# Talking-heads attention with a soft mixture of experts: another order of the mixing, the row transfers, the copies and the projection

## The chip, the cores and the metric

The kernel runs on one core of a Trainium2 chip. The metric is the device time of one execution in microseconds (us); lower is better. The engines are PE (TensorE: matmuls, with PEld for its weight loads), DVE (VectorE), ACT (ScalarE), POOL (GpSimd) and SP (SyncE, which here only issues transfers).

## The reference

There are 4 sequences of 2048 tokens with 256 features. The attention has 16 heads of 16 features and mixes the heads twice, once before the softmax and once after it. A soft mixture of experts follows; both have a residual and a norm behind them. The change touches the attention alone:

```python
qkv = x @ Wqkv.T + bqkv
q, k, v = jnp.split(qkv, 3, axis=-1)
...
q = apply_rope(q)
k = apply_rope(k)
logits = jnp.einsum('bhid,bhjd->bhij', q, k) * SCALE
logits = jnp.einsum('bhij,gh->bgij', logits, Wpre)
attn = jax.nn.softmax(logits, axis=-1)
attn = jnp.einsum('bhij,gh->bgij', attn, Wpost)
out = jnp.einsum('bhij,bhjd->bhid', attn, v)
out = out.transpose(0, 2, 1, 3).reshape(b, n, DIM)
return out @ Wout.T + bout
```

## The kernel before

For each sequence the kernel computes q, k and v (`qkv`), then the attention, then the experts (`moe`). All data is float32.

**The attention** takes the queries by pairs of blocks. A block has 8 queries (`IB`), so with 16 heads it fills 128 partitions; a pair `n` has two blocks, `x` = 0 and 1, and there are 128 pairs a sequence. The keys are split into two halves, `j` = 0 and 1, of 1024 (`HALF`), and into four quarters of 512 (`QN`).

A pair passes through four stages, spread over several steps of the loop in line 562:

1. `raw_banks(n, c, engs)`, lines 359 to 382: the products of q and k, before any mixing. It runs twice for a pair, for `c` = 0 and 1 (8 heads each). PE writes four PSUM tiles `s` (line 374). Each is copied into the SBUF tile `raw` by one of the functions that it returns: `fs[0]` to `fs[3]`. `V` copies on DVE (line 550), `S_` on ACT (line 553). `pair_q` (line 351) prepares the q side on POOL.
2. `raw_rows(n)`, lines 384 to 396: eight transfers on SP's queue of 256 KB each. They bring `raw` into four row tiles `raws[n][j][x]`, in which the heads lie on partitions. Row tiles have 10 buffers (`ROWS`), `raw` has two.
3. `logits(n, j)`, line 414: PE mixes the heads into two PSUM tiles `l`, one for each `x`. `top(n, j, x)`, line 429, takes the negative maximum of a row on DVE, and `expo(n, j, x)`, line 438, the exponential on ACT, back into the row tile, with the sum beside it. A maximum belongs to one half of the keys alone, so `shares(n)`, lines 444 to 457, works out the factors that join the halves: `m` on DVE (line 449), a subtraction on POOL (451), an exponential on ACT (452), a product and a sum on POOL (454, 456). `weights(n)`, lines 459 to 472, takes the reciprocal on DVE (463) and makes the mixing weights `w` from it on POOL (464, 466).
4. `mix(n, x, j, engs)`, line 495: PE mixes the heads again and turns the result at once, into two PSUM tiles `t` for one `x` and one `j`. `V` and `S_` copy them into `aT`. When 32 queries (four blocks, `GI`) are there, `values(grp, hf)`, line 519, multiplies with v in two parts, `hf` = 0 and 1, each in a step of its own, into a PSUM tile `o`. Two DVE instructions copy it (530, 531). After every fourth group, so in every eighth step, `finish(it)`, lines 537 to 547, projects 128 queries: it loads x (line 259, on SP's queue), adds the bias on POOL (540), multiplies on PE into `pz` (543), and adds and takes the statistics of the norm on DVE (546, 237).

**One step `n`** holds, for each half `j`: `logits(n, j)`, `raw_banks(n + 2, j, ...)`, the maxima and exponentials of pair `n`, and the mixing of pair `n - 1`. At its end it starts the row transfers of pair `n + 2` and multiplies with v for an earlier group.

[...]the tiles `l` have two buffers of two banks, and all the others (`s`, `t`, `o`, `pz`) share four buffers of one bank.

**The order of the work.** A scheduler places each instruction on its engine's queue by its own estimate of when the inputs are ready, so an instruction can stand elsewhere than the program has it. `keep(...)` stops that for one instruction: it stays behind everything that the program has before it on that engine. Before the change the copies `V` and `S_`, `top`, `expo` and the row transfers are kept; `shares`, `weights`, the copies of `o` and `finish` are not. PE's and POOL's instructions are placed freely in both kernels.

Of the kernel before, what the change touches and what calls it, by code (L numbers as in the profile page):

```python
# [16 lines left out]
P = 128  # L17
# [8 lines left out]
def kernel(  # L26
# [301 lines left out]
    def attention(b, y, qT, kT, v):  # L328
# [30 lines left out]
        def raw_banks(n, c, engs):  # L359
# [3 lines left out]

            if c == 0:
                raws[n] = {
                    "qb": pair_q(n),
                    "from": work.tile([P, HP, QN], F32, tag="raw", name=f"raw_{b}_{n}"),
                }
            qb = raws[n]["qb"]
            prs = [ps_t.tile([P, QN], F32, tag="t", name=f"s_{b}_{n}_{c}_{r}") for r in range(4)]  # L370
            for r in range(4):
                rows = slice(32 * r, 32 * (r + 1))
                for q in range(4):
                    nc.tensor.matmul(  # L374
                        prs[r][32 * q : 32 * (q + 1), :],
                        qb[rows, c, q % 2].rearrange("p s i h x -> p (s i h x)"),
                        kT[rows, c, ts(q, QN)],
                        start=True,
                        stop=True,
                    )  # L380
# [3 lines left out]
        def raw_rows(n):  # L384
# [7 lines left out]
            for x in range(2):  # L392
                for q in range(2):
                    for j in range(2):
                        p0 = 32 * (2 * j + q)
                        keep(nc.sync.dma_start(raws[n][j][x][:, ts(q, QN)], raw[p0 + x : p0 + 32 : 2]))  # L396
# [47 lines left out]
        def shares(n):  # L444
# [4 lines left out]
            nc.vector.tensor_tensor(m, m2[:, :, 0:1], m2[:, :, 1:2], ALU.min)  # L449
            f = small.tile([P, 2, 2], F32, tag="f", name=f"f_{b}_{n}")  # L450
            nc.gpsimd.tensor_tensor(f, m.to_broadcast([P, 2, 2]), m2, ALU.subtract)  # L451
            nc.scalar.activation(f, f, AF.Exp)  # L452
# [6 lines left out]
        def weights(n):  # L459
# [3 lines left out]
            nc.vector.reciprocal(z, z)  # L463
# [45 lines left out]
        outT = {}  # L509

        def values(grp, hf):
# [18 lines left out]
            nc.vector.tensor_copy(dst, po[:, 0, :])  # L530
            nc.vector.copy_predicated(dst, odd, po[:, 1, :])
            if hf == 1:
                aT.pop(grp)
                if part == P // GI - 1:
                    finish(it)

        def finish(it):
            oT = outT.pop(it)
            xt = load_x(b, it, "xr")
            nc.gpsimd.tensor_add(xt, xt, bout_sb)  # L540
# [5 lines left out]
            nc.vector.tensor_add(y[:, it, :], pz[:, :D], xt)  # L546
            norm_stats(y[:, it, :], it, st)
# [14 lines left out]
        for n in range(n_pairs + 3):  # L562
# [4 lines left out]
            for j in range(2):  # L567
# [7 lines left out]
                fs[0]()  # L575
                fs[1]()
# [3 lines left out]
                fs[2]()  # L580
                fs[3]()
                if cur:
                    expo(n, j, 1)
                if prv:
                    mix(n - 1, j, 0, (V, S_))
                    mix(n - 1, j, 1, (V, S_))
                    if j == 1:
                        state.pop(n - 1)
                if j == 1:
# [4 lines left out]
            if cur:  # L594
                shares(n)
        mv, rstd = norm_finish(st, f"a{b}")
# [190 lines left out]
```

## Time and profile before

| | us |
|---|---|
| median of 3 runs | 10179.63 |
| lowest, highest | 10157.14, 10192.11 |
| the profiled execution | 10203.34 |
| its span, first to last instruction | 10201.3 |

The granted clock of TensorE is 0.937 on average.

| engine | busy us | share of the span | instructions |
|---|---|---|---|
| PE | 7866.9 | 77% | 264788 |
| PEld | 5049.5 | 49% | 264788 |
| DVE | 5577.1 | 55% | 9074 |
| ACT | 4927.5 | 48% | 9758 |
| POOL | 1617.7 | 16% | 6478 |

The transfers of SP's queue take 44.6% of the time of the 16 DMA engines, and the queues that bring instructions 1.4% and 0.1%.

The profile names instructions by line, engine, output and inputs. A line of the timeline has the start, the duration, what ran and how often; in brackets behind it stand the idle time of that engine just before and what ended it. "issue" there means that the engine waited for nothing that the profile shows. A line of the list of waits has the engine with the work that waited, what it waited for, the sum in us, how often, and the longest. Each float32 matmul is recorded as two matmuls and two weight loads.

### The profile page before, as it was taken

How to read it: one execution, taken by the hardware profiler on the slowest of the kernel's cores; microseconds unless marked ns; L12 is line 12 of the kernel's file. 1: busy time of each engine (PE TensorE's matmuls, PEld its weight loads, DVE VectorE, ACT ScalarE, POOL GpSimd, SP SyncE). 2: the span in 40 equal slices, each digit the busy share in tenths (PEclk: the TensorE clock that was granted, in tenths of full speed). 3: DMA queues.
4: the chain of work that ended last, by engine and by line, in shares of the span. 5: the costliest groups of instructions: out<-in, count | busy, mean ns of one | idle time of the engine just before them, and what ended most of it. 6: DMA issues, size and time to landing. Idle time of an engine off the chain costs nothing. (4 is left out here: it accounts for less than half of the span.)

```text
span 10201.3 us, 569636 instructions
## 1 busy us (share of the span) xinstructions
PE 7866.9 (77%) x264788; PEld 5049.5 (49%) x264788; DVE 5577.1 (55%) x9074; ACT 4927.5 (48%) x9758; POOL 1617.7 (16%) x6478
## 2 busy tenths in 40 slices
PE   7887778776778787777677877787767787777776
PEld 4554555454455454545444545555544554545554
DVE  5555555554555555555455555555545555555554
ACT  3544555453455455545345545554534554555453
POOL 2111111111211111111121111111112111111111
PEclk9989999998999999999899999999989998999898
DMA  4444554452455454545244545554514554555441
GB/s 108 120 120 111 129 128 121 113 124 57 105 122 124 115 127 121 124 116 120 54 105 120 124 115 124 124 126 117 123 48 113 120 124 115 125 124 124 116 120 47
DMA packets 653638, 1150.99 MB, mean 113 GB/s; under 512 B 95616, under 2 KB 125440, under 8 KB 651264
## 3 DMA queue, kind: packets, MB, share of 16 engines
q1 hardware_dynamic: 616704, 1099.18, 44.6%
q8 instruction: 2076, 34.01, 1.4%
q10 hardware_dynamic: 34560, 15.36, 0.6%
q14 instruction: 298, 2.44, 0.1%
HBM read 32.13 MB, written 8.39 MB: 4 GB/s over the span
## 5 line engine op out<-in xcount | busy, mean ns | idle before, releaser
L495 PE MATMUL t<-w,rows 64*64 64x64 f32 x131072 | 3029.9, 233 | 877.9 <-ACT raw L553 566.4
L495 PEld LDWEIGHTS t<-w,rows 64*64 64x64 f32 x131072 | 2600.5, 144 | 2156.1 <-ACT raw L553 1067.5
L553 ACT COPY raw<-s 128x512 f32<-128x512 f32 x2552 | 1443.0, 589 | 3977.5 <-PE s L374 3460.3
L429 DVE TENSOR_REDUCE m<-l 128x1 f32<-128x1024 f32 x2048 | 2496.9, 1220 | 869.4 <-PE l L414 869.2
L438 ACT ACTIVATE rows<-l,m 128x1024 f32<-128x1024 f32 x2048 | 2311.7, 1129 | 111.9 <-DVE m L429 110.6
L374 PE MATMUL s<-kT,qb 32*32 32x512 f32 x32768 | 2029.2, 639 | 177.7 <-issue 162.1
L414 PE MATMUL l<-rows,wmix_sb 32*32 32x512 f32 x32768 | 1630.0, 636 | 307.3 <-issue 275.1
L550 DVE COPY aT<-t 128x512 f32<-128x512 f32 x2048 | 1359.0, 683 | 508.3 <-PE t L495 506.2
L519 PE MATMUL o<-aT,v 128*32 128x64 f32 x65536 | 1155.5, 223 | 619.4 <-issue 439.7
L519 PEld LDWEIGHTS o<-aT,v 128*32 128x32 f32 x65536 | 1006.4, 111 | 740.6 <-issue 500.6
L553 ACT COPY aT<-t 128x512 f32<-128x512 f32 x2048 | 1179.5, 601 | 395.2 <-PE t L495 381.0
L550 DVE COPY raw<-s 128x512 f32<-128x512 f32 x1544 | 1056.9, 685 | 524.9 <-PE s L374 512.8
L374 PEld LDWEIGHTS s<-kT,qb 32*32 32x32 f32 x32768 | 715.0, 106 | 979.1 <-issue 707.4
L351 POOL TENSOR_TENSOR qb<-qT,hmask 128x16 f32<-128x16 f32 (+3 forms) x3584 | 647.3, 220 | 1899.9 <-PE s L374 1899.9
L451 POOL TENSOR_TENSOR f<-m,m 128x4 f32<-128x4 f32 x512 | 101.7, 199 | 4532.3 <-DVE m L449 4531.5
L463 DVE RECIPROCAL z<-z 128x2 f32<-128x2 f32 x512 | 85.0, 166 | 1149.6 <-POOL z L456 1149.6
L414 PEld LDWEIGHTS l<-rows,wmix_sb 32*32 32x32 f32 x32768 | 328.9, 106 | 672.3 <-issue 513.4
L530 DVE COPY aoT<-o 128x32 f32<-128x32 f32 x512 | 98.3, 192 | 957.6 <-PE o L519 957.6
L438 ACT ACTIVATION_READ_ACCUMULATOR rows<-l,m 128x1 f32 x2048 | 433.5, 212 | 0.0
L466 POOL TENSOR_TENSOR w<-wblk_sb,f 128x256 f32<-128x256 f32 x512 | 313.7, 613 | 40.6 <-POOL f L464 1.0
L454 POOL TENSOR_TENSOR zf<-f,z 128x4 f32<-128x4 f32 x512 | 102.4, 200 | 751.9 <-ACT f L452 751.9
L309 POOL TENSOR_TENSOR s<-qk,wq 128x256 f32<-128x256 f32 x128 | 116.3, 928 | 494.1 <-DVE qk L293 481.4
(122 smaller groups left out, 2620.9 us busy)
## 6 DMA issues: line engine op xcount, KB each, us to landing
rows<-raw SPq DMA_DIRECT2D x4096, 256.0 KB
x<-in_x_dram SPq DMA_DIRECT2D x64, 128.0 KB
xr<-in_x_dram SPq DMA_DIRECT2D x64, 128.0 KB
out_dram<-qT SPq DMA_DIRECT2D x16, 512.0 KB
wm<-in_w_dram ACTq DMA_DIRECT2D x8, 512.0 KB
wm<-in_w_dram ACTq DMA_DIRECT2D x4, 1024.0 KB
wq<-in_wqkvT_dram ACTq DMA_DIRECT2D x4, 768.0 KB
wq<-in_bqkv_dram ACTq DMA_DIRECT2D x4, 384.0 KB
```

The source lines that it names most:

```text
L309: nc.gpsimd.tensor_mul(s[:, :, a, :], qk[:, :, 1 - a, :], ss[a])
L351: nc.gpsimd.tensor_tensor(qb[:, :, g, s0:s1, :, :, x].rearrange("p c s i h -> p c (s i) h"), qT[:, t, :, i0:i1].unsqueeze(3).to_broadcast( ...
L374: nc.tensor.matmul(prs[r][32 * q : 32 * (q + 1), :], qb[rows, c, q % 2].rearrange("p s i h x -> p (s i h x)"), kT[rows, c, ts(q, QN)], sta ...
L414: nc.tensor.matmul(pls[x][32 * c : 32 * (c + 1), ts(h, 512)], wmix_sb[32 * q : 32 * (q + 1), :], raws[n][j][x][32 * q : 32 * (q + 1), ts(h ...
L429: nc.vector.tensor_reduce(s["m2"][:, x, j : j + 1], s["l", j][x], AX.X, ALU.max, negate=True)
L438: nc.scalar.activation(s["e", j][x], s["l", j][x], AF.Exp, bias=s["m2"][:, x, j : j + 1], accum_out=s["z2"][:, x, j : j + 1],)
L454: nc.gpsimd.tensor_tensor(zf, f, z2, ALU.mult)
L466: nc.gpsimd.tensor_tensor(w, wblk_sb.rearrange("p g i -> p (g i)").unsqueeze(1).to_broadcast([P, 4, HEADS * IQ]), f.rearrange("p x j -> p ...
L495: nc.tensor.matmul(pts[r][64 * c : 64 * (c + 1), a, :], e[rows, k0 : k0 + 64], s["w"][rows, 2 * x + j, :], start=True, stop=True,)
L519: nc.tensor.matmul(po[32 * c : 32 * (c + 1)].rearrange("p a i -> p (a i)"), v[:, t, g0 * HD : (g0 + 2) * HD], at[:, t, g0 : g0 + 2, :].rea ...
L550: keep(nc.vector.tensor_copy(dst, src))
L553: keep(nc.scalar.copy(dst, src))
```

## The change

It has five parts.

- The q k products of `raw_banks` lie on other partition groups: the key quarters 0, 2, 1, 3 instead of 0, 1, 2, 3. `raw_rows` fits that and sends all of `j` = 0 first, then `j` = 1; before, all of `x` = 0 went first.
- The mixing of a half step takes both blocks `x` for one half `j`; before, it took one block for both halves.
- All four copies `fs` stand ahead of the first exponential and the second maximum. The first `mix` of a half step now stands between the two exponentials.
- More of the attention is kept in program order: `m` and the exponential of `shares`, the reciprocal of `weights`, the copies of `o`, and the addition and statistics of `finish`.
- `finish` runs in the middle of the step after the one whose `values` complete its 128 queries. Its load of x and the addition of the bias move into `values`, two steps ahead of it.

```diff
             for r in range(4):
                 rows = slice(32 * r, 32 * (r + 1))
                 for q in range(4):
                     nc.tensor.matmul(
                         prs[r][32 * q : 32 * (q + 1), :],
-                        qb[rows, c, q % 2].rearrange("p s i h x -> p (s i h x)"),
-                        kT[rows, c, ts(q, QN)],
+                        qb[rows, c, q // 2].rearrange("p s i h x -> p (s i h x)"),
+                        kT[rows, c, ts(2 * (q % 2) + q // 2, QN)],
...
-            for x in range(2):
-                for q in range(2):
-                    for j in range(2):
-                        p0 = 32 * (2 * j + q)
-                        keep(nc.sync.dma_start(raws[n][j][x][:, ts(q, QN)], raw[p0 + x : p0 + 32 : 2]))
+            for j in range(2):
+                for x in range(2):
+                    for h in range(2):
+                        p0 = 32 * (2 * h + j) + x
+                        keep(
+                            nc.sync.dma_start(
+                                raws[n][j][x][:, ts(h, QN)], raw[p0 : p0 + 31 : 2]
+                            )
+                        )
...
-            nc.vector.tensor_tensor(m, m2[:, :, 0:1], m2[:, :, 1:2], ALU.min)
+            keep(nc.vector.tensor_tensor(m, m2[:, :, 0:1], m2[:, :, 1:2], ALU.min))
...
-            nc.scalar.activation(f, f, AF.Exp)
+            keep(nc.scalar.activation(f, f, AF.Exp))
...
-            nc.vector.reciprocal(z, z)
+            keep(nc.vector.reciprocal(z, z))
...
-            nc.vector.tensor_copy(dst, po[:, 0, :])
-            nc.vector.copy_predicated(dst, odd, po[:, 1, :])
+            keep(nc.vector.tensor_copy(dst, po[:, 0, :]))
+            keep(nc.vector.copy_predicated(dst, odd, po[:, 1, :]))
+            if part == P // GI - 1 and hf == 0:
+                xs[it] = load_x(b, it, "xr")
+                nc.gpsimd.tensor_add(xs[it], xs[it], bout_sb)
             if hf == 1:
                 aT.pop(grp)
                 if part == P // GI - 1:
-                    finish(it)
+                    todo.append(it)
 
         def finish(it):
             oT = outT.pop(it)
-            xt = load_x(b, it, "xr")
-            nc.gpsimd.tensor_add(xt, xt, bout_sb)
...
-            nc.vector.tensor_add(y[:, it, :], pz[:, :D], xt)
-            norm_stats(y[:, it, :], it, st)
+            keep(nc.vector.tensor_add(y[:, it, :], pz[:, :D], xs.pop(it)))
+            keep(nc.vector.bn_stats(st[:, it, :], y[:, it, :]))
...
                 if cur:
                     top(n, j, 0)
-                fs[0]()
-                fs[1]()
+                for f in fs:
+                    f()
                 if cur:
                     expo(n, j, 0)
                     top(n, j, 1)
-                fs[2]()
-                fs[3]()
+                if prv:
+                    mix(n - 1, 0, j, (V, S_))
                 if cur:
                     expo(n, j, 1)
                 if prv:
-                    mix(n - 1, j, 0, (V, S_))
-                    mix(n - 1, j, 1, (V, S_))
+                    mix(n - 1, 1, j, (V, S_))
                     if j == 1:
                         state.pop(n - 1)
-                if j == 1:
+                if j == 0:
+                    while todo:
+                        finish(todo.pop())
+                else:
                     if nxt:
                         raw_rows(n + 2)
                     if val:
                         values(grp, hf)
             if cur:
                 shares(n)
+        while todo:
+            finish(todo.pop())
```

More of the change, by code (lines that the diff above doesn't have):

```diff
@@ L507, in mix @@
                 )
-        outT = {}
+        outT, xs, todo = {}, {}, []
         def values(grp, hf):
```

## The prediction

> **What bounds the kernel now.** I read the page's totals first. No engine is full, and the busiest, PE at 77%, is a modelled figure; the chain that ended last is a mixture.
>
> ```profile
> PE 7866.9 (77%) x264788; PEld 5049.5 (49%) x264788; DVE 5577.1 (55%) x9074; ACT 4927.5 (48%) x9758; POOL 1617.7 (16%) x6478
> ...
> q8 instruction: 2076, 34.01, 1.4%
> ...
> PE 13%; ACT 6%; issue 3%; DVE 1%; DMA 0%; POOL 0%; SPq 0%; ACTq 0%; POOLq 0%; DVEq 0%
> ```
>
> So I went to one step (one pair of query blocks) in the timeline. In it l, s, t, o are PE's matmuls of lines 414, 374, 495, 519.
>
> ```profile
> 1049.36 1.14 PE L414 MATMUL l<-rows,wmix_sb 32*32 32x512 f32 x32
> 1050.24 1.54 PE L374 MATMUL s<-kT,qb 32*32 32x512 f32 x32
> 1050.55 1.23 DVE L429 TENSOR_REDUCE m<-l 128x1 f32<-128x1024 f32 x1 [0.67 <-PE l L414]
> ...
> 1052.22 1.36 PE L495 MATMUL t<-w,rows 64*64 64x64 f32 x64 [0.44 <-ACT raw L553]
> ...
> 1059.42 0.25 DVE L449 TENSOR_TENSOR m<-m 128x2 f32<-128x2 f32 x1
> ...
> 1061.87 0.17 DVE L463 RECIPROCAL z<-z 128x2 f32<-128x2 f32 x1 [2.19 <-POOL z L456]
> ...
> 1062.84 0.34 PE L495 MATMUL t<-w,rows 64*64 64x64 f32 x5 [1.67 <-issue]
> ...
> 1063.10 1.97 PE L519 MATMUL o<-aT,v 128*32 128x64 f32 x123
> ...
> 1066.86 0.31 PE L519 MATMUL o<-aT,v 128*32 128x64 f32 x5 [1.78 <-issue]
> ...
> 1067.10 1.14 PE L414 MATMUL l<-rows,wmix_sb 32*32 32x512 f32 x32
> 1067.22 0.19 DVE L530 COPY aoT<-o 128x32 f32<-128x32 f32 x1 [3.44 <-PE o L519]
> ```
>
> The step goes from one l to the next: 17.74 us. PE stands twice for 1.7 us in front of a few last matmuls, with nothing to wait for ("issue"). The distance from the one point to the other is 128 matmuls with 128 weight loads, 256 instructions. Over the run PE has 529,576 instructions and the instruction queue 2,076 packets: 255 each. So these are waits for the next block of instructions. In the trace's packet records PE resumes 1.43 us after a packet's end (median of 914 stalls over 1 us; quartiles 1.34 and 1.51), a packet takes 1.1 us, and the next one starts 1.2 us after PE enters a block when the row transfers are quiet, 2.3 us when they fill the DMA engines. A block therefore costs at least 3.7 us, 4.9 us beside transfers. A step has four: a **floor of 15 to 19 us**, while the step is 17.97 on average (from the start of one exponential to that of the next pair's). All such stalls over 0.6 us make 1,936 us, 3.7 us a step. PE's own stream, by offsets in this step without its stalls, would need 14.5 us.
>
> The block edges move by about four instructions a step, so periods swing between 16 and 20 us twice a batch. Last, the list of waits:
>
> ```profile
> DVE z L463 <- POOL z L456: 1149.6, 512, 2.3
> PEld t L495 <- issue: 924.3, 827, 2.5
> ...
> PE t L495 <- ACT raw L553: 566.4, 1823, 1.1
> ...
> PE o L519 <- ACT aT L553: 174.6, 352, 0.7
> ...
> DVE qT L546 <- PE pz L543: 130.9, 64, 3.7
> ```
>
> [...]
>
> **The change, part by part.** Offsets are from the start of l.
>
> *All four q k copies ahead of the second maximum.* Before, DVE runs maximum (1.19 to 2.42), copy, maximum, copy; the second t begins fully at 4.80, and in the second half at 10.8, where the first t ended at 4.22 and 10.1: about 0.6 us of PE each. With the copies (0.68 on DVE, 0.58 on ACT) in front, the second t follows the first. The price: the second maximum and its exponential, which frees the bank of the next l, come some 0.66 us later. In the first half that takes the gain back; in the second there is slack until the next step's l.
>
> *Pinning.* The planner had put m (L449) and the reciprocal (L463) ahead of the t copies, where DVE stood 2.2 us for POOL. Gone: copies come at once, o's buffer is free some 0.5 us sooner. **Late instead**: m is now behind the two o copies, at the end of the step, and the reciprocal, with all its wait, ahead of the next step's first maximum. Worked out: o ends at 0; copies to 0.53; m to 0.71; subtraction on POOL (0.20) to 0.99; exponential on ACT (0.23) to 1.29; product and sum on POOL (0.20, 0.19, 0.08 between) to 1.84; reciprocal (0.17) to 2.05. Behind it waits the first maximum: 1.96 instead of 1.19, 0.77 later. POOL then makes w (0.20 and 0.61): 3.0, where t starts at 2.86 now. With one of its banks emptied by a DVE copy behind that maximum, t waits to 3.9. So 0.2 to 0.95 us on PE, zero when a fetch stall lies in l or s. Both parts together take PE's own stream from 14.5 to about 13.9 us.
>
> *What the floor leaves of it.* The second half's 1.1 us fall into blocks that mostly wait for fetch: I take 0.3 us in 40% of 512 steps, −60 us (bounds 0 and −560). The late chain lengthens the block from l to t, which before was near the floor (4.3 us): 0.4 us in the 40% of the steps whose block edge is late in t, **+82 us** (bounds 0 and +0.95 × 512 = +486).
>
> *Halves.* Mixing takes both x of one key half instead of both halves of one x: the same 128 t records, and in both orders two row buffers come free per half step. The q k products only exchange partition groups. The eight row transfers keep their size (256 KB, 0.55 us each of SP); per half step one was issued after the first t and three after the second, now two and two, and the transfers needed first go first. Rows hardly end a wait of PE (its l waited 12.2 us for them in all; the 291.7 us that ACT's copies are listed as waiting for them end 1.34 us after s starts, as in every step, so there it was s). What can change is their meeting with fetches: 54% of the stalled fetches were asked for under load over 0.6, at 1.1 us each. I take −0.2 us a step, **−100 us**; bounds −0.5 and +0.3 a step (−256, +154), since edges may meet them worse.
>
> *Projection a step later.* A finishing step is 2.17 us longer than its neighbours (60 of them): o copies, pz, addition and statistics stand in front of l and the maximum. Moved to the middle of the next step, its four PE records (0.7 us) stand between t and l, where PE waits for the exponential anyway; addition (0.43) and statistics (0.43) delay a maximum. I take 0.7 left: 64 × 1.5, **−94 us** (bounds −140, 0). Its load (128 KB, on SP, ahead of the next row transfers) and the addition of the bias (0.73, POOL) go up two steps. POOL waits 7 us each for that load now (398.1 us, 57 times) in its idle time; in front of the m chain it would cost up to 7 × 64 = 448 us. I take nothing, as the buffer is free long before.
>
> The sum: −60 + 82 − 100 − 94 = −172 us. Against the profiled execution (10203.34 us; span 10201.3) that is 10,031; it stood 0.23% above the median of 10179.63, so about **10,010** in the median.
>
> **Rivals.** *Late chain decides (slower).* If planner and bank order make t wait for the DVE copy in nearly every step, with fetch edges seldom in l and s, the chain costs 0.85 us × 512 = +435 instead of +82: +181, **10,360**. It decides from 254/512 = 0.5 us a step on. For it: fast steps (16.3 us) have their edge late in t, without room. Against: in slow steps the stall stands in l and hides it. *Floor gives way (much faster).* PE's full 0.6 us a step, −307, with projection and transfers: −500, **9,680**. For it: less collision lowers the floor itself; against: four fetches a step stay. *The floor takes all.* Everything shorter becomes "issue", and the chain eats the projection's gain: within 0.3%, **10,180**; for it, that nothing here removes a PE instruction.
>
> **How the numbers follow.** Likeliest (0.43): 10,010, own range 9,900 to 10,120. Late chain 0.30, floor gives way 0.20, floor takes all 0.07. So faster 0.63, same 0.07, slower 0.30; 0.3% is about what can be told from no change. The range 9,740 to 10,430 leaves out the outer tails of both rivals, one in ten each.
>
> **What the profile would show.** Right: the wait of the reciprocal for POOL stays near 1.1 to 1.5 us but stands ahead of the maximum of line 429 (before: ahead of the copies); the wait of POOL's subtraction is for m after o; "PE t for ACT raw" and "PE o for ACT aT" fall; finishing steps are under 1 us longer than others; issue waits stay in the thousands of us over PE and PEld. Wrong: first t starting at 3.9 or later in most steps, or PE's l waiting for the second exponential by over 1 us; then the late chain has won. If the instruction waits fell by half, my floor was no floor.

## The result: slower by 2.9%

The changed kernel took a median of 10462.51 us (4 runs, 10458.99 to 10489.34); the kernel before, on the same chip, 10179.83 us. The ratio is **1.0286, 95% interval 1.0261 to 1.0311** (the two medians alone give 1.0278, inside it). The profiled execution took 10489.34 us, its span is 10487.6 us; that is 286 us more than the span before.

The page's totals, instruction queue and chain after:

```profile
PE 7726.9 (74%) x264788; PEld 5032.2 (48%) x264788; DVE 5573.7 (53%) x9074; ACT 4998.6 (48%) x9758; POOL 1616.0 (15%) x6478
...
q8 instruction: 2080, 34.08, 1.3%
...
PE 63%; issue 19%; ACT 9%; DVE 4%; POOL 3%; DMA 2%; SPq 1%; ACTq 0%; another core or an unknown queue 0%; DVEq 0%; POOLq 0%
```

The same instructions ran, with the same busy times to 2%, and as many instruction packets. So the change added waits, not work. The clock view shows another difference: the mean granted clock fell from 0.937 to 0.917.

```profile
core 0: 10487.6 us, clock 0.917
```

Two waits of PE before, for the comparison:

```profile
PE o L519 <- issue: 439.7, 371, 3.7
...
PEld t L495 <- POOL w L466: 2.8, 2, 1.4
```

The list of waits after (who waited for what, sum in us, times, longest):

```profile
DVE aoT L535 <- PE o L524: 1791.3, 512, 5.6
...
PEld o L524 <- issue: 955.0, 503, 3.8
PEld t L500 <- issue: 953.1, 770, 2.5
PE o L524 <- issue: 882.4, 503, 3.7
...
DVE z L468 <- POOL z L461: 673.2, 512, 5.5
...
PEld t L500 <- POOL w L471: 331.9, 198, 4.0
PE t L500 <- ACT raw L559: 314.9, 697, 1.5
...
PE o L524 <- ACT aT L559: 38.7, 140, 1.2
```

The waits for copies fell as forecast ("PE t for ACT raw" from 566.4 to 314.9, "PE o for ACT aT" from 174.6 to 38.7). What rose is the wait for instructions **inside o**, from 439.7 us in 371 stalls to 882.4 in 503: from 1.19 to 1.75 us each. New is t waiting for w.

One step of the timeline after, from one l to the next (19.3 us):

```profile
1050.99 1.22 PE L419 MATMUL l<-rows,wmix_sb 32*32 32x512 f32 x32
1051.12 0.19 DVE L535 COPY aoT<-o 128x32 f32<-128x32 f32 x1 [4.40 <-PE o L524]
...
1051.45 0.17 DVE L454 TENSOR_TENSOR m<-m 128x2 f32<-128x2 f32 x1
...
1053.61 0.17 DVE L468 RECIPROCAL z<-z 128x2 f32<-128x2 f32 x1 [2.00 <-POOL z L461]
1053.70 1.20 DVE L434 TENSOR_REDUCE m<-l 128x1 f32<-128x1024 f32 x1
...
1054.14 0.61 POOL L471 TENSOR_TENSOR w<-wblk_sb,f 128x256 f32<-128x256 f32 x1
...
1054.80 0.33 PE L500 MATMUL t<-w,rows 64*64 64x64 f32 x4 [1.39 <-POOL w L471]
...
1064.94 1.21 PE L524 MATMUL o<-aT,v 128*32 128x64 f32 x71
...
1068.77 1.61 PE L524 MATMUL o<-aT,v 128*32 128x64 f32 x57 [2.62 <-issue]
...
1070.31 2.09 PE L419 MATMUL l<-rows,wmix_sb 32*32 32x512 f32 x32
```

Three things stand here. The late chain runs as predicted: o's copy, m, the factors, the reciprocal at 1053.61 with 2.00 us of waiting, only then the first maximum; w ends at 1054.75 and t starts behind it, 3.8 us into the step. The stall in o is 2.62 us, not 1.8. And the l that follows takes 2.09 us, where the same 32 records took 1.22 us a step before: they run at half the clock (granted 0.50 from 1070.31 to 1072.40, 1.00 in the l of the step before). The view by windows (us, busy time of PE with its count, granted clock, DMA share, GB/s) shows both ends of that stall:

```profile
1064.90:1066.20 1.30, 1.24 (x77) 1.00 0.93 192
1068.75:1070.40 1.65, 1.64 (x65) 0.58 0.14 41
```

PE enters a block with 57 records of t at 1063.92; in the window right behind, the DMA engines are 93% busy. By the packet records, the packet with the next block starts 2.46 us after PE enters and takes 0.96 us; PE goes on 1.43 us behind its end, at 1068.77. That is 4.85 us in all, near the 4.9 us that the prediction had for a block beside transfers. Half clock begins 0.25 us after PE goes on, at 1069.02, and lasts 3.41 us.

**The clock is a part that the prediction left out.** The trace's clock records have two values, 1.0 and 0.5. In the kernel before, 227 stretches are at half clock; the shortest lasts 3.41 us, and 142 of them last just that. This length is called a window below. Of PE's gaps in the kernel before, these were followed by half clock within two windows (6.83 us) of their start: 46 of 240 between 1 and 1.5 us, 60 of 92 between 2 and 2.5 us, 29 of 34 above 2.5 us. (A moment taken at random is, in 15 cases of 100. Eight gaps of over 7 us, outside the attention, are not counted here or below.) The share is not fixed: in the changed kernel it is 100 of 216 between 2 and 2.5 us. After, there are 142 gaps above 2.5 us instead of 34, and 1751 us at half clock instead of 1297.

What these 454 us more of half clock cost can only be estimated. At half clock the 32 records of an l take 2.09 us, at full clock 1.22 (medians before); so 0.42 of the time at half clock is lost, 189 us, if PE is the bound throughout. The 111 runs of the kernel before in these experiments say less: per us of lost clock (half of the time at half clock) they differ by 0.52 us of time, with a correlation of 0.77, which makes 118 us. By these estimates the clock has 118 to 189 of the 286 us, and the longer waits have the rest.

### The profile page after: what moved, and what is told of

It is laid out like the page before. It is cut to its first block, busy times and chain, and to the rows that moved or that the text cites. A ratio compares the mean times of both kernels' runs of the same rounds, so it can differ in the third digit from the quotient of the medians.

```text
span 10487.6 us, 570647 instructions
## 1 busy us (share of the span) xinstructions
PE 7726.9 (74%) x264788; PEld 5032.2 (48%) x264788; DVE 5573.7 (53%) x9074; ACT 4998.6 (48%) x9758; POOL 1616.0 (15%) x6478
## 4 chain that ended last, share of the span: by engine, by line
PE 63%; issue 19%; ACT 9%; DVE 4%; POOL 3%; DMA 2%; SPq 1%; ACTq 0%; another core or an unknown queue 0%; DVEq 0%; POOLq 0%
PE t L500 21%; PE l L419 15%; PE s L375 12%; PE o L524 10%; ACT raw L559 5%; ACT rows L443 2%; POOL qb L351 2%; DVE raw L556 1%; PE pqk L283 1%; DMA xr<-in_x_dram 1%; ACT aT L559 1%; PE pf L717 1%; PE pz L549 1%; PE l_d L191 1%; DMA rows<-raw 1%
## 5 line engine op out<-in xcount | busy, mean ns | idle before, releaser
L500 PEld LDWEIGHTS t<-w,rows 64*64 64x64 f32 x131072 | 2486.3, 148 | 2078.8 <-issue 953.1
L500 PE MATMUL t<-w,rows 64*64 64x64 f32 x131072 | 2733.7, 236 | 942.6 <-issue 413.3
L559 ACT COPY raw<-s 128x512 f32<-128x512 f32 x2552 | 1357.7, 591 | 2251.4 <-PE s L375 2166.5
L375 PE MATMUL s<-kT,qb 32*32 32x512 f32 x32768 | 2114.1, 665 | 205.3 <-issue 181.2
L419 PE MATMUL l<-rows,wmix_sb 32*32 32x512 f32 x32768 | 1789.5, 654 | 337.6 <-issue 309.9
L524 PE MATMUL o<-aT,v 128*32 128x64 f32 x65536 | 1183.9, 224 | 924.5 <-issue 882.4
L559 ACT COPY aT<-t 128x512 f32<-128x512 f32 x2048 | 1214.6, 593 | 428.7 <-PE t L500 422.8
L556 DVE COPY raw<-s 128x512 f32<-128x512 f32 x1544 | 1020.7, 685 | 634.1 <-PE s L375 598.2
L375 PEld LDWEIGHTS s<-kT,qb 32*32 32x32 f32 x32768 | 761.2, 108 | 950.2 <-issue 678.2
L457 ACT ACTIVATE f<-f 128x4 f32<-128x4 f32 x512 | 105.3, 206 | 1972.3 <-POOL f L456 1972.3
L419 PEld LDWEIGHTS l<-rows,wmix_sb 32*32 32x32 f32 x32768 | 375.9, 107 | 825.9 <-issue 520.0
L468 DVE RECIPROCAL z<-z 128x2 f32<-128x2 f32 x512 | 85.0, 166 | 673.2 <-POOL z L461 673.2
## 6 DMA issues: line engine op xcount, KB each, us to landing
rows<-raw SPq DMA_DIRECT2D x4096, 256.0 KB
```

Of the source, the lines that this page charges most:

```text
L375: nc.tensor.matmul(prs[r][32 * q : 32 * (q + 1), :], qb[rows, c, q // 2].rearrange("p s i h x -> p (s i h x)"), kT[rows, c, ts(2 * (q % 2) ...
L419: nc.tensor.matmul(pls[x][32 * c : 32 * (c + 1), ts(h, 512)], wmix_sb[32 * q : 32 * (q + 1), :], raws[n][j][x][32 * q : 32 * (q + 1), ts(h ...
L457: keep(nc.scalar.activation(f, f, AF.Exp))
L500: nc.tensor.matmul(pts[r][64 * c : 64 * (c + 1), a, :], e[rows, k0 : k0 + 64], s["w"][rows, 2 * x + j, :], start=True, stop=True,)
L524: nc.tensor.matmul(po[32 * c : 32 * (c + 1)].rearrange("p a i -> p (a i)"), v[:, t, g0 * HD : (g0 + 2) * HD], at[:, t, g0 : g0 + 2, :].rea ...
L556: keep(nc.vector.tensor_copy(dst, src))
```

## The experiments

In all tables the ratio is against the kernel before, run on the same chip in the same rounds; half clock, the mean step (from the exponential of a pair to that of the next) and the gaps come from the trace of each profiled execution. The experiments ran on several chips, where the kernel before took 10146 to 10172 us in the median, so the ratios are to be compared and not the medians.

### The order in which the row transfers are issued

Two theories stood against each other: the price is in the halves, whose transfers collide worse with the instruction fetches; or it is in the late chain. The halves alone, in the kernel before:

```diff
-                        qb[rows, c, q % 2].rearrange("p s i h x -> p (s i h x)"),
-                        kT[rows, c, ts(q, QN)],
+                        qb[rows, c, q // 2].rearrange("p s i h x -> p (s i h x)"),
+                        kT[rows, c, ts(2 * (q % 2) + q // 2, QN)],
...
+            for j in range(2):
+                for x in range(2):
+                    for h in range(2):
...
-                    mix(n - 1, j, 0, (V, S_))
-                    mix(n - 1, j, 1, (V, S_))
+                    mix(n - 1, 0, j, (V, S_))
+                    mix(n - 1, 1, j, (V, S_))
```

> The kernel before with one part of the change alone: the q k products on their new partition groups, the row transfers by halves of the keys, and mixing by halves (both mixings still behind the second exponential). Late chain theory: within 1.5% of before, 10,030 to 10,330 us. Transfer theory: the loss is here, 10,400 to 10,650 us, with more issue time of PE.

The same with one loop exchanged, so that successive transfers write to two row tiles in turn, as before the change; and that one exchange in the changed kernel:

```diff
             for j in range(2):
-                for x in range(2):
-                    for h in range(2):
+                for h in range(2):
+                    for x in range(2):
```

> The kernel before with partition groups and mixing by halves of the keys, but the transfers issued in turn to the two blocks x. Theory of the transfers' order and the clock: 10,140 to 10,230 us, where the same kernel with the new order took 10,385, with half-clock time near the 1,297 us of before. Rival (mixing or groups): 10,350 to 10,400 us.

> The changed kernel with the row transfers of a key half issued in turn to the two blocks x (loops j, h, x in place of j, x, h), so that again one transfer goes after the first t of a half step and three after the second, as before the change. Theory (the transfers that follow the first t at once meet the fetch of the next instruction block, the stall in o grows to over 2.5 us, the granted clock of PE is halved for a window of 3.4 us[...]): 10,230 to 10,330 us, half-clock time down from 1,751 to about 1,400 us. Rival (mixing by halves or the new partition groups are to blame, not the order of issue): 10,420 to 10,480 us, half-clock time as it was.

The opposite test leaves everything in the kernel before and exchanges its two inner loops, so that each row tile is written by two transfers in succession; in the second form with the other half of the keys first, `for j in (1, 0)`:

```diff
             for x in range(2):
-                for q in range(2):
-                    for j in range(2):
+                for j in range(2):
+                    for q in range(2):
```

> The kernel before with the order of issue of its eight row transfers alone changed: loops x, j, q in place of x, q, j, so that two go after the first t of a half step and two after the second (before: one and three). Transfer theory: the whole loss of the halves is in this order, 10,310 to 10,400 us, PE's gaps of 2.5 us and more rise from 34 to over 120 and half-clock time from 1,297 to about 1,650 us. Rival (it needs mixing by halves too): 10,120 to 10,200 us.

> The kernel before with the opposite order of issue: the tile freed by the second t first (x, j = 1 then 0, q), so that none of the eight transfers can go after the first t and four go after the second. Transfer theory: the fetch asked for at the end of t meets an empty DMA, stalls in o shrink below those of before (1.2 us on average), 10,050 to 10,150 us. Rival: the four transfers then meet the fetches in l and s, and the rows come later: 10,180 to 10,350 us.

| kernel | median us | ratio [95%] | half clock us | step us | gaps over 2.5 us |
|---|---|---|---|---|---|
| before | – | 1 | 1297 | 17.97 | 34 |
| after | 10462.51 | 1.0286 [1.0261, 1.0311] | 1751 | 18.50 | 142 |
| b_halves | 10384.55 | 1.0217 [1.0189, 1.0244] | 1656 | 18.35 | 159 |
| b_halves_abab | 10181.15 | 1.0027 [1.0015, 1.0038] | 1174 | 17.83 | 36 |
| a_abab | 10307.17 | 1.0151 [1.0131, 1.0171] | 1502 | 18.18 | 71 |
| b_aabb | 10529.19 | 1.0355 [1.0319, 1.0390] | 1833 | 18.64 | 201 |
| b_bbaa | 10527.65 | 1.0352 [1.0320, 1.0383] | 1717 | 18.58 | 194 |

**The order of eight transfers decides 140 to 360 us.** It alone makes the kernel before 3.5% slower; it is worth 1.9% with the halves alone and 1.3% in the changed kernel. With the order in turn the halves cost 0.3%, close to nothing. The direction was expected for b_aabb, the size was not: it lies above both ranges named, and so does b_bbaa (below). The timelines show how. First the end of a step in b_halves, SP's issues and PE:

```profile
1048.01 1.19 SPq L397 DMA_DIRECT2D rows<-raw  x2
...
1049.70 0.34 PE L499 MATMUL t<-w,rows 64*64 64x64 f32 x5 [0.63 <-issue]
...
1049.96 1.97 PE L523 MATMUL o<-aT,v 128*32 128x64 f32 x123
...
1054.27 0.31 PE L523 MATMUL o<-aT,v 128*32 128x64 f32 x5 [2.33 <-issue]
```

Then one of b_halves_abab with its block edge at the same place:

```profile
1054.00 0.55 SPq L397 DMA_DIRECT2D rows<-raw  x1
...
1055.36 0.34 PE L499 MATMUL t<-w,rows 64*64 64x64 f32 x5 [0.29 <-issue]
...
1055.70 1.97 PE L523 MATMUL o<-aT,v 128*32 128x64 f32 x123
...
1059.37 0.31 PE L523 MATMUL o<-aT,v 128*32 128x64 f32 x5 [1.70 <-issue]
```

Behind the first t one row tile is free. When two successive transfers go into it, both start at once; when they alternate, the second waits for the next t, and the rest with it (three are issued from 1055.73 on). PE enters a block at the five t records, and the packet with the next block starts behind that place. With two transfers under way it takes 4.57 us until PE goes on (1049.70 to 1054.27), with one 4.01 us. The same stall is 2.33 or 1.70 us.

The whole run shows the same. In 1,004 of the 1,024 half steps, two transfers follow the first t and two the second in b_halves; in b_halves_abab it is one and three. For the stalls of over 1 us in o, the block's packet starts 2.45 us after PE has entered the block before it in b_halves (median of 235), 1.42 us in b_halves_abab (of 228). The packet then takes 0.98 and 0.96 us, and PE goes on 1.44 us behind it in both. So the later start of the fetch is what makes this stall longer. The waits of o in each run (b_halves, then b_halves_abab):

```profile
PE o L523 <- issue: 600.4, 350, 3.4
```

```profile
PE o L523 <- issue: 439.4, 359, 3.7
```

That is 1.72 against 1.22 us a stall, 161 us in all. All instruction stalls over 0.6 us grow by less, from 1,943 (before) to 2,008 us (b_halves). They are counted here on the weight loads, from one start to the next, where an instruction packet had ended 1.1 to 2 us before; some lie under matmuls that still run. So a part of what o's stall gains is spared elsewhere. But of the gaps between 1.5 and 2 us in the kernel before, half clock followed 78 of 210, of those between 2 and 2.5 us 60 of 92 (in b_halves 47 of 101 and 69 of 116): the stall has grown into a range that half clock follows more often. Half-clock time rises by 359 us from before to b_halves; by the two estimates above that is worth 93 to 149 us, of 196 between the two spans (10397.6 and 10201.3). So the clock is perhaps half of the loss or more; no run separates it from the longer stall that comes before it. b_bbaa was to have no early transfer at all. Its trace shows again two after the first t, presumably since the buffers are handed out in the order of issue and not by half; that case stays untried.

### The late chain, and what stands in front of it

b_pins puts the late chain into the kernel before: `keep` on m, on the exponential of `shares`, on the reciprocal, and on the two copies of o, nothing else. a_early takes the chain's price away in the changed kernel by giving `shares` its turn before `values`, so that m needn't wait for o.

```diff
-            nc.vector.tensor_tensor(m, m2[:, :, 0:1], m2[:, :, 1:2], ALU.min)
+            keep(nc.vector.tensor_tensor(m, m2[:, :, 0:1], m2[:, :, 1:2], ALU.min))
...
-            nc.scalar.activation(f, f, AF.Exp)
+            keep(nc.scalar.activation(f, f, AF.Exp))
...
-            nc.vector.reciprocal(z, z)
+            keep(nc.vector.reciprocal(z, z))
...
-            nc.vector.tensor_copy(dst, po[:, 0, :])
-            nc.vector.copy_predicated(dst, odd, po[:, 1, :])
+            keep(nc.vector.tensor_copy(dst, po[:, 0, :]))
+            keep(nc.vector.copy_predicated(dst, odd, po[:, 1, :]))
```

> The kernel before with one part of the change alone: m and the exponential of shares, the reciprocal of weights and the two o copies are kept in program order. Late chain theory: the whole loss is here, and without the gain of the projection it is larger than the change's: 10,430 to 10,650 us, with w as a releaser of t. Transfer theory: within 1% of before, 10,080 to 10,280 us. Fetch floor theory: 10,200 to 10,350 us.

```diff
+                    if cur:
+                        shares(n)
                     if val:
                         values(grp, hf)
-            if cur:
-                shares(n)
```

> The changed kernel with one edit: shares(n) is called ahead of values(grp, hf), so that m is kept ahead of the two o copies instead of behind them. Late chain theory (the m-to-w chain starts only after o and holds back maximum, t and the next l): the loss goes and the rest of the change shows, 9,950 to 10,180 us; POOL's w ends hardly any wait of t (466 us over PE and PEld in the changed kernel). Transfer theory (the new order of mixing and row transfers meets the instruction fetches worse): the chain was off the path, so 10,380 to 10,480 us as in the changed kernel (10,462). Fetch floor theory (PE waits for instruction blocks, whatever stands between): what is gained on t comes back as issue, 10,300 to 10,460 us.

b_pins: 10243.47 us, ratio 1.0080 [1.0058, 1.0102]. a_early: 10355.58 us, 1.0197 [1.0167, 1.0228], 0.9% under the changed kernel by the two ratios. The chain is real and costs about 80 us; it isn't the main part. Its half-clock time is 1456 us, 159 more than before, which by the two estimates is worth 41 to 66 of the 80 us. The waits of b_pins:

```profile
DVE z L463 <- POOL z L456: 560.9, 512, 2.3
...
PEld t L495 <- POOL w L466: 393.4, 254, 3.0
```

t waits for w 254 times in 512 steps; in the kernel before 2 times, for 2.8 us in all. Then both repairs (`shares` early, transfers in turn) together, and the same with copies, exponentials and mixing in the order of before as well:

> The changed kernel with both repairs: shares ahead of the values and the transfers in turn. If the two losses are separate and add: 10,150 to 10,230 us, so the rest of the change (copies ahead of the second maximum, projection later, mixing by halves) gains about nothing over before. If they are one loss (both only lengthen the same stall in o): 10,280 to 10,330 us. If the rest gains what the prediction gave it: 9,950 to 10,080 us.

```diff
-                for f in fs:
-                    f()
+                fs[0]()
+                fs[1]()
                 if cur:
                     expo(n, j, 0)
                     top(n, j, 1)
-                if prv:
-                    mix(n - 1, 0, j, (V, S_))
+                fs[2]()
+                fs[3]()
                 if cur:
                     expo(n, j, 1)
                 if prv:
+                    mix(n - 1, 0, j, (V, S_))
                     mix(n - 1, 1, j, (V, S_))
```

> The changed kernel with both repairs (shares ahead of the values, transfers in turn: 10,263 us) and the copies, exponentials and mixings in the order of before. If the later second maximum costs what is left over: 10,120 to 10,180 us. If the pins cost it, wherever shares stands: 10,240 to 10,290 us.

a_early_abab: 10263.22 us, 1.0096 [1.0068, 1.0125]. a_rep_oldcopies: 10241.00 us, 1.0090 [1.0064, 1.0116]. Neither comes back to 1: an early m doesn't make an early w. In a_rep_oldcopies PE's t still waits 64 times for w, 103.3 us in all. One step of its timeline shows what is in front of w there:

```profile
1059.95 2.69 POOL L351 TENSOR_TENSOR qb<-qT,hmask 128x24 f32<-128x24 f32 x15
...
1062.59 0.20 POOL L469 TENSOR_TENSOR f<-f,z 128x4 f32<-128x4 f32 x1
...
1062.87 0.61 POOL L471 TENSOR_TENSOR w<-wblk_sb,f 128x256 f32<-128x256 f32 x1
...
1063.54 3.07 PE L500 MATMUL t<-w,rows 64*64 64x64 f32 x128 [2.16 <-POOL w L471]
```

POOL's burst of small instructions for `pair_q` stands ahead of the factor and w, and PE waits 2.16 us. The view begins at 1060 us, so its first line has only the last 15 of the burst; the whole has 35 and takes 6.21 us, from 1056.43 on. The other repair, no `keep` on m, the exponential and the reciprocal, leaves them where the scheduler puts them. Against a_abab:

```diff
-            keep(nc.vector.tensor_tensor(m, m2[:, :, 0:1], m2[:, :, 1:2], ALU.min))
+            nc.vector.tensor_tensor(m, m2[:, :, 0:1], m2[:, :, 1:2], ALU.min)
...
-            keep(nc.scalar.activation(f, f, AF.Exp))
+            nc.scalar.activation(f, f, AF.Exp)
...
-            keep(nc.vector.reciprocal(z, z))
+            nc.vector.reciprocal(z, z)
```

> The changed kernel without its two losing parts: transfers in turn to the two blocks, and m, the exponential of shares and the reciprocal of weights not kept in order. If the loss is these two and nothing else, the rest (copies ahead -0.3%, projection -0.3%, groups and mixing by halves +0.3%) gives -0.3%: 10,080 to 10,150 us, and w hardly ends a wait of t. If the kept o copies, or the parts together, cost something more: 10,200 to 10,300 us.

a_abab_unpin: 10226.32 us, 1.0063 [1.0038, 1.0088], against 1.0151 with these three kept.

### Projection, copies, and the rest

b_finish moves the projection alone (todo list, load and bias in `values`, `keep` on addition and statistics). b_copies2 has all four copies ahead and the first mixing between the exponentials, but mixes by blocks.

```diff
+            if part == P // GI - 1 and hf == 0:
+                xs[it] = load_x(b, it, "xr")
+                nc.gpsimd.tensor_add(xs[it], xs[it], bout_sb)
...
-                    finish(it)
+                    todo.append(it)
...
-                if j == 1:
+                if j == 0:
+                    while todo:
+                        finish(todo.pop())
+                else:
```

> The kernel before with one part of the change alone: the projection runs in the middle of the next step, with its addition and statistics kept in order, its load of x and addition of the bias two steps ahead. If the prediction's step is right (1.5 us off 64 finishing steps): 10,060 to 10,120 us, and finishing steps are under 1 us longer than the others. If the load's wait on POOL takes it back, as the 625 us of that wait in the changed kernel would allow: 10,150 to 10,250 us.

```diff
-                fs[0]()
-                fs[1]()
+                for f in fs:
+                    f()
...
-                fs[2]()
-                fs[3]()
+                if prv:
+                    mix(n - 1, j, 0, (V, S_))
...
-                    mix(n - 1, j, 0, (V, S_))
```

> The kernel before with one part of the change alone: all four q k copies ahead of the first exponential and second maximum, and the first mixing of a half step between the exponentials. Theory of separate parts (order of issue +1.9%, pins +0.8%, projection -0.3%, partition groups and mixing by halves +0.3%): what is left for this part is +0.2%, 10,130 to 10,220 us. If the later second maximum is what the repaired kernel (shares ahead, transfers in turn) still loses: +0.7 to +1.2%, 10,230 to 10,290 us, and PE's l waits for the exponential. If the prediction's gain on t is real: 10,080 to 10,120 us.

b_finish: 10125.13 us, 0.9970 [0.9958, 0.9983]. A finishing step before is 19.44 us, 2.17 longer than its neighbours; now it is the step behind it, 18.55 against 17.55. So 1.0 us is left, not 0.7. In POOL's queue the addition of the bias now waits longer for its load (398.1 us before):

```profile
POOL xr L534 <- DMA xr<-in_x_dram: 924.1, 58, 20.3
```

That this takes a part of the gain is not shown: t's weight loads wait for w only 3 times in b_finish, 4.2 us in all.

b_copies2: 10119.39 us, 0.9974 [0.9963, 0.9984]. Waits of t for copies fall in it (566.4 to 387.1 us), and waits of o for instructions rise (from 439.7 us in 371 stalls to 677.2 in 496), so the gain in t goes into o's stalls there, and yet the kernel is a little faster.

The parts add up to 2.17 + 0.80 − 0.30 − 0.26 = 2.41%, not 2.86. The last run tells which two don't fit: a_abab_unpin with copies, exponentials and mixing in the old order (the diff shown for a_rep_oldcopies), so the halves in turn, the later projection and the kept copies of o are what is left of the change.

> The changed kernel with the row transfers alternating between two row tiles, with the minimum, its exponential and the reciprocal placed freely, and with the copies, exponentials and mixing in the order of before. What is left of the change is the mixing by halves and the later projection. The same kernel with all copies ahead measured 1.0063 [1.0038, 1.0088], although its parts alone measured +0.27 (halves, alternating), -0.26 (copies ahead) and -0.30 per cent (projection). Theory 1: the copies ahead fit the mixing by halves badly, and this loses their gain or more; then this kernel is near the sum of the other two, about 1.000 (0.997 to 1.003). Theory 2: the later projection fits the mixing by halves badly; then the order of the copies does nothing or its own 0.26 per cent, and this kernel is at 1.006 to 1.009.

10172.82 us, 1.0004 [0.9994, 1.0014]. The copies ahead, worth −0.26% in the kernel before, cost +0.6% on top of these parts; which of them doesn't go with the copies was not tried. The same kernel also shows what the three keeps cost: a_rep_oldcopies (1.0090) differs from it only in having them, with `shares` early, so they cost 0.9% even so. The waits of a_abab_unpin_oldcopies, and then those of a_abab_unpin:

```profile
PE t L500 <- ACT raw L559: 565.5, 1833, 1.0
...
PE o L524 <- issue: 417.2, 349, 3.1
```

```profile
PE o L524 <- issue: 634.8, 462, 3.7
...
PE t L500 <- ACT raw L559: 384.2, 826, 1.6
```

t waits 181 us less for copies, o 218 us more for instructions: that gain turns into fetch stalls. But b_copies2 shows nearly the same exchange and is faster. What differs is half-clock time: here it rises from 1254 to 1379 us, there it hardly moves (1297 to 1275). Why is open. This gives **a path from before to after in measured steps**: halves in alternating order, later projection and kept copies of o 1.0004; all copies ahead 1.0063; m, exponential and reciprocal kept 1.0151; transfers two and two 1.0286.

### The clock, and a faster kernel

b_mix128 tests the block of 256 instructions (before, 531,451 instructions of PE, the 1,875 that are neither matmul nor weight load among them, in 2,076 packets: 256.0 each): it makes the second mixing with one 64x128 weight where there were two of 64x64, so a step has 768 instructions instead of 1024. b_filler adds one useless 128x128x448 matmul ahead of each o, into columns that nobody reads, to see whether the clock follows PE's work.

```diff
-                    for c in range(2):
-                        k0 = a * P + 64 * c
-                        nc.tensor.matmul(
-                            pts[r][64 * c : 64 * (c + 1), a, :],
-                            e[rows, k0 : k0 + 64],
...
+                    nc.tensor.matmul(
+                        pts[r][:, a, :],
+                        e[rows, ts(a, P)],
```

> The kernel before with the second mixing in half as many matmuls: one of 64 x 128 in place of two of 64 x 64 side by side, same columns streamed, same results. PE has 768 instructions a step in place of 1024, three blocks in place of four. Fetch floor theory: a block less a step, so the step falls from 18.0 us towards PE's own 14.5 us, 8,500 to 9,200 us, and the issue time of PE falls by more than half. If PE's own streaming or the copies set the step instead: 9,900 to 10,300 us.

```diff
             po = ps_t.tile([P, 512], F32, tag="t", name=f"o_{b}_{grp}_{hf}")
+            nc.tensor.matmul(
+                po[:, 2 * GI :], ident, wout_sb.rearrange("p c n -> p (c n)")[:, 2 * GI :],
+                start=True, stop=True,
+            )
```

> The kernel before with more work: one useless matmul of 128 x 128 x 448 into the free columns of the o bank ahead of each o, 2 more PE records (4 instructions) and some 0.6 us of PE a step. Clock theory[...]: [...]half-clock time falls from 1,297 to 700 to 1,100 us and the time to 9,950 to 10,180 us although PE has more to do[...]. If the clock follows something else, the added work costs 0.2 to 0.6 us a step: 10,280 to 10,480 us.

Both edits in one kernel, then the fewer instructions with the later projection, and with a_abab_unpin:

> The kernel with the second mixing in half as many matmuls (9,954 us, 1,878 us of it at half clock, steps of 15.5 us at full clock), with one useless matmul of 448 columns ahead of each o. Clock theory: the added work costs up to 0.6 us a step (310 us) and takes away half-clock time; if that falls below 1,200 us, the time is 9,700 to 9,950 us.[...]

> A candidate to beat both kernels: the kernel before with the second mixing in half as many matmuls (9,954 us) and the projection in the middle of the next step (-0.3% by itself). If the two add: 9,880 to 9,960 us. If the half-clock windows (1,878 us) grow with the added wait, as with the filler: over 10,050 us.

> The same with the second mixing in half as many matmuls, the best single edit so far (-2.0%). If it adds: 9,860 to 9,960 us. If its half-clock windows (1,878 us on the kernel before) grow, over 10,000 us.

| kernel | median us | ratio [95%] | half clock us | step us | gaps over 2.5 us |
|---|---|---|---|---|---|
| b_filler | 10140.65 | 0.9990 [0.9973, 1.0007] | 905 | 17.92 | 18 |
| b_mix128 | 9953.76 | 0.9807 [0.9761, 0.9852] | 1878 | 17.64 | 12 |
| b_mix128_filler | 10985.20 | 1.0786 [1.0736, 1.0837] | 2755 | 19.49 | 15 |
| b_mix128_finish | 9939.65 | 0.9796 [0.9768, 0.9825] | 1751 | 17.46 | 11 |
| a_abab_unpin_mix128 | 9956.83 | 0.9792 [0.9762, 0.9823] | 1830 | 17.51 | 13 |

The filler takes 392 us of half clock away, and the time is the same: its own work, and what it moves, pays for what the clock gives. It also halves the gaps over 2.5 us (18 for 34) and cuts o's waits for instructions from 439.7 to 164.7 us, so it doesn't tell whether the clock follows the work in the gaps or the gaps themselves.

b_mix128 cuts the instruction stalls, counted as above, from 1,943 to 458 us and is **2% faster than the kernel before**; with the later projection, or in the changed kernel without its two losing parts (transfers two and two, the three keeps), it is the same within the intervals. It gains far less than the stalls it removes. If instruction blocks were what bounds a step, it was to take 8,500 to 9,200 us; 9,954 is in the range named for PE's own work or the copies as the bound. Its groups (busy, mean ns of one, then idle before and its causes) and its clock:

```profile
L493 PE MATMUL t<-w,rows 64*128 64x64 f32 x65536 | 4454.3, 289 | 448.2 <-ACT raw L551 433.7 <-DVE raw L548 9.6 <-issue 1.8
...
L493 PEld LDWEIGHTS t<-w,rows 64*128 64x128 f32 x65536 | 4308.6, 202 | 1448.8 <-ACT raw L551 837.1 <-issue 573.6 <-DVE raw L548 15.4
```

```profile
core 0: 10030.0 us, clock 0.906
```

A weight load takes 202 ns where the 64x64 one took 144, so 64 records of t take 3.9 to 4.07 us where 128 took about 2.9: PE is busy with t for 4454.3 us instead of 3029.9. And the clock is at half for 1878 us with hardly a long gap left. In the windows before its half-clock stretches the longest gap is under 0.6 us in the median. With the filler half clock grew to 2755 us. One wait in b_mix128 was not tried: ACT's copies of s are listed as waiting for row transfers for 1014.1 us, where it was 291.7 before. The cause stays open.

## Why the prediction was wrong

The forecast was 10,010 us, faster with a chance of 0.63; the result, 10462.51, lies above the range too.

**The step that failed is "Halves".** It took the exchange of "one early, three late" for "two and two" as a slight relief, −100 us, with +154 as the worst case. Alone it measured +2.17% (+221 us on that group's median before of 10163.82), and in turn, without the exchange, only +0.27%. The observation behind it was right: two transfers issued earlier, and fetches delayed by load. But the estimate spread them over a step. The fetch that ends in o follows PE's entry into a block near the end of t, right behind the two early transfers: it starts 2.45 us after that entry in b_halves, instead of 1.42 with one early transfer in b_halves_abab, and o's stalls grow from 439.4 to 600.4 us. The step also had **no term for the clock**, where 359 us more at half clock are worth 93 to 149 us by the estimates above. The reading "granted clock 0.937" was at hand and wasn't asked what lowered it. In the changed kernel this exchange is the largest of the measured steps, 1.3 of 2.9%; the keeps have 0.9 and the copies ahead 0.6.

**The late chain**: +82 us forecast, +80 measured with the pins alone (which also include the gain from the stall removed). The size is right in part by luck, for the forecast priced a longer wait alone, and half or more of the 80 us can be the clock. As the rival that decides, 10,360, it would have had to cost 435 us; it doesn't. What the step missed lies on POOL: behind the reciprocal the factor and w stand in a queue with `pair_q`, which no edit of the chain's start gets round.

**Copies and stall, −60.** The copies alone, without the stall that the pins remove, gave −27 us. That part of it would become "issue" was said; that it would be a loss of about 0.6% beside the other parts of the change was not.

**Projection, −94.** It gave −24 us between medians: 1.2 us of the 2.17 remain in the changed kernel (19.42 us where its neighbours take 18.2), 1.0 in b_finish, against 0.7 assumed. With 1.0 left the finishing steps alone would give 64 × 1.17 = 75 us; where the other 50 went is not shown. The cover named for the addition of the bias, POOL's idle time, was there but small: the wait for the load rose from 398.1 to 625.3 us in the changed kernel.

```profile
POOL xr L539 <- DMA xr<-in_x_dram: 625.3, 55, 15.3
```

**The block of instructions** is a real wait, but that it is the bound is not shown. b_mix128 takes a quarter of PE's instructions in a step away and these stalls fall from 1,943 to 458 us, yet the time falls by 2%; its own t and half clock grew, so it doesn't disprove the floor either. The prediction read its 1,936 us as time that PE stands. The count comes out only on the weight loads; PE's matmuls wait for "issue", over 0.6 us at a time, for 1,012 us. In the changed kernel the stalls rose to 2,679 us.

**The signs named.** The reciprocal's wait (673.2 / 512 = 1.31 us, ahead of the maximum) and the two waits for copies came as forecast. PEld's wait in front of l for the second exponential was to show the late chain; it rose, but with the copies ahead and not with the chain. Before, after, and in b_copies2, which has no late chain:

```profile
PEld l L414 <- ACT rows L438: 36.7, 20, 3.2
```

```profile
PEld l L419 <- ACT rows L443: 185.7, 249, 2.9
```

```profile
PEld l L414 <- ACT rows L438: 231.1, 302, 3.0
```

In b_pins, which has the chain and not the copies, it is 33.0 us in 18 waits. The test "first t at 3.9 us or later in most steps" was badly set too: it holds for about 60% of the steps before and nearly 70% after.

## What to carry to other kernels

Where the fetch of an instruction block starts later beside transfers (2.45 us after PE enters a block in b_halves, 1.42 in b_halves_abab), look up at which instruction PE enters each block, and keep the start of transfers off that place: the order of eight issues was worth 1.3 to 3.5% here, with the same bytes and the same work. Read the granted clock beside the stalls: half clock followed gaps of 2 to 2.5 us more often than shorter ones here (60 of 92, against 46 of 240 between 1 and 1.5 us), so a longer stall may cost more than its length. A pin frees one queue by fixing another, so follow the pinned chain through every engine it passes before it is counted as free, and measure edits together as well as alone: the copies ahead gained 0.26% alone and lost 0.6% beside other parts.

## What was not expected of the hardware

- Half clock came after gaps well under the 3.41 us that its shortest stretch lasts: after 60 of 92 gaps between 2 and 2.5 us in the kernel before.
- The packets of the row transfers (2 KB each) took a mean 135 ns before, 129 in b_halves and 130 after, 142 in b_aabb and a_abab, 140.5 in b_halves_abab; so both the groups and the order of issue count. With two and two the groups of the change are the faster ones (129 against 142); in turn they are the slower ones (140.5 against 135). That may be why two and two costs the halves 1.9% and the kernel before 3.5%; no run separates that.
- A 64x128 weight load took 202 ns against 144 for 64x64, in means that hold half-clock stretches too.
